# A graph layer and a top-p attention layer on one core: tile ends newest first in the tail, one search cut moved from ACT to DVE, three adjacency loads held back by a memset

## The chip, the cores and the metric

The kernel runs on one core of one Trainium2 chip. The metric is the device time of one execution in microseconds, the median of the runs shown. Engines are named as in the profile: PE (TensorE, with its weight loads PEld), ACT (ScalarE), DVE (VectorE), POOL (GpSimd), SP (SyncE, which here only issues DMAs).

## The reference

Node features `x` are 3327 x 256 in f32, and `adj` is a 3327 x 3327 matrix of zeros and ones with about four ones to a row. Two layers follow each other, each with a layernorm over its sum with its input.

```python
# layer 0: attention over neighbours, then a GRU cell
Wh  = h @ W
e   = leaky_relu(Wh @ a[:F] + (Wh @ a[F:]).T, 0.2)
att = softmax(where(adj > 0, e, NEG_INF), axis=1)
gi, gh = (att @ Wh) @ w_ih.T + b_ih, h @ w_hh.T + b_hh
...                                     # r, z, n of a GRU cell
x = layernorm(x + (1 - z) * n + z * h)

# layer 1: two steps of top-p attention beside a fixed propagation R
R = adj + eye(N); R = R / R.sum(-1, keepdims=True)
Xf = Xa = X = x
for n in range(2):
    A  = top_p_attention(Xa, W1, W2, W3)   # softmax of a 64-wide bilinear form, largest
                                           # entries of a row up to a sum of 0.9, renormalised
    Xf = R @ Xf
    Xa = A @ Xa
    Z  = Z + Xf @ U1[n].T + Xa @ U2[n].T
x = layernorm(X + layernorm(X + Z) * ln_g + ln_b)
```

The second argument `S` of layer 1 is `adj`. So `R @ Xf` is a gather of a few neighbours per row, while the attention is dense: 3327 logits per row, of which the largest up to nine tenths of the row's sum are kept.

## The kernel before, in words

Rows are handled in 26 tiles of 128 (`NT`), the last of 127. `P` is 128, `D` 256.

**Layer 0.** `run` (L1035 on) first projects all tiles (`project`, up to L768): x is loaded and turned, multiplied by W, and the result is stored to DRAM by ACT's queue as `whx`, the table that later gathers read. `ds` (L763) is the last POOL instruction of a tile there. Beside the projection the rows of `adj` are loaded and searched. `load_adj(t, queue)` (L807) brings tile t into one of three arrays `ad[t % 3]` in two transfers, three blocks of 832 columns (1248 KB) and one of 831 (415 KB). `neighbours(t)` (L814) finds the ones with FIND_INDEX8 on DVE (L819); when a tile has been searched, tile t + 3 goes on the list `wanted`. `advance` (L1056) is one phase of the written-out order: it runs some finds, issues one wanted load on SP if the phase is above `NT - EARLY` = 13, opens a tile every sixth phase (`EVERY`) and moves every open tile one step. `tile` (from L840) takes the neighbour lists of a tile, computes where its edges lie (`half` L868, `square` L870, `mid` L875, `edge` L908) and gathers five blocks of 128 rows of `whx` (L613) before attention and GRU.

**Layer 1.** An item is a tile in a step, 52 in all. `product` (L1731) multiplies the masked attention of item i with Xa, seven groups of four 128-wide blocks; behind each group the functions put in a slot (`slot(g, f, ...)`) are issued, which is how logits, exponentials, search and mask of the coming item are woven in. The order on PE, ACT, DVE and in layer 0 on POOL is the order of issue in the program; the remaining instructions are ordered by a scheduler with priorities from the program order.

A row whose list of largest candidates doesn't suffice is "left over": its position, bias and sums are stored (`left_over`, L1531), and three sets of up to 128 such rows, "hard sets" 0, 1 and 2, are worked off at the end. The parts of a hard set k:

- `hard_load` (L1536) loads its rows' numbers and gathers its inputs (L1552).
- `hard_q` (L1558) makes its query on PE and ACT (L1563, L1565) and a first upper threshold `top` (L1571).
- `hard_exp` (L1574) makes its 3327 exponentials.
- `coarse_bound` (L1587) lowers `top` once for each cut factor: four ACT passes over half a row each (L1602), then eight small POOL instructions (L1608 to L1617, the next cut's L1597).
- `bound` (L1621) does the same on DVE: one pass of `kept_sum` (L1341) and three small instructions per cut (L1629, L1632, L1634).
- `hard` (L1638) is the search proper on DVE: one pass (L1644), 20 MAX8 (L1213), a sort, three drops with MATCH_REPLACE8 (L1335), one pass (L1673) and the reciprocal `rA` (L1676). It has eight yields.
- `hard_end` (L1679) is the attention product and the output of the set, mainly PE.
- `hard_store` (L1706) scatters the 128 finished rows to the output (L1708).

The six cut factors are `CUTS` = 1/16, 1/4, 1/2, 0.71, 0.84, 0.92. Sets 1 and 2 use the first three (`COARSE`) coarsely on ACT and the others on DVE; set 0 uses two on ACT and four on DVE.

**The tail.** `ends` (L1744) begins behind the last product. `tile_end(t)` (L1462) turns and multiplies the four propagated inputs of a tile on PE (L1181, L1440), adds x through an identity product (L1492), and hands the PSUM tile to `output_rows` (L1445): a copy to `h` (L1448), two layernorms, each with `moments` on DVE (L1383, L1385) and POOL (L1386, L1387) and three ACT instructions (L1393 to L1395), and two POOL instructions between them (L1453, L1455). The buffers `h`, `x1`, `xb` are twelve slots of 256 columns in the memory of `qT`, no longer needed. `tick()` opens one tile end and moves every open one on by one step, oldest first. `more()` moves the head of `queue` (start or end of a hard set), runs a tick, and gives each coarse bound two steps. The search of the sets is the loop of `ends`: for k = 0, 1, 2 the bounds, then `hard(k)`, with one `more()` at each yield; when all sets are through, `more()` runs until nothing is left.

Of the kernel before, what the change touches and what calls it, by code (L numbers as in the profile page):

```python
# [9 lines left out]
F32 = mybir.dt.float32  # L10
# [6 lines left out]
P = 128  # L17
# [630 lines left out]
class Layer0:  # L648
# [186 lines left out]
    def tile(self, t):  # L835
# [25 lines left out]

        nc.gpsimd.tensor_scalar(info[:r, 0:1], info[:r, 0:1], 1.0, None, ALU.max)
        yield from to(2)
        pst = self.ps.tile([P, 512], F32, tag="sm", name=f"pst{t}")
        nc.tensor.matmul(pst[:, 0:1], sh.lower16, d16, start=True, stop=True)
# [4 lines left out]
        nc.gpsimd.tensor_scalar(square, d1, d1, 0.25, ALU.mult, ALU.mult)  # L870
        nc.gpsimd.tensor_copy(a[:, :MAXDEG], info[:, :MAXDEG])
# [163 lines left out]
    def run(self):  # L1035
# [20 lines left out]
        def advance(finds):  # L1056
            nonlocal phase
            for _ in range(finds):
                find()
            if self.wanted and phase > NT - EARLY:  # L1060
                self.load_adj(self.wanted.pop(0), nc.sync)
            if phase % EVERY == 0 and phase // EVERY < NT:
                tiles.append(self.tile(phase // EVERY))
            for g in list(tiles):
                if next(g, True):
                    tiles.remove(g)
                    self.done += 1
            next(logits, None)
            phase += 1
# [53 lines left out]
class Layer1:  # L1123
# [321 lines left out]
    def output_rows(self, pz, terms, h, r, tag):  # L1445

        nc = self.nc
        nc.scalar.copy(h, pz[:r, :D])  # L1448
        yield
        m = self.moments(h, r, f"a{tag}")  # L1450
        yield
        self.normalized(h, h, m, r, f"a{tag}")
        nc.gpsimd.tensor_tensor(h, h, self.g[:r], ALU.mult)  # L1453
        for term in terms:
            nc.gpsimd.tensor_tensor(h, h, term, ALU.add)  # L1455
        yield
        yield
        m = self.moments(h, r, f"b{tag}")
        yield
        self.normalized(h, h, m, r, f"b{tag}")  # L1460

    def tile_end(self, t):  # L1462
# [3 lines left out]
        a = self.work.tile([P, EB, P], F32, tag="m", name=f"xfs{t}").rearrange("p b c -> p (b c)")  # L1466
        xa2 = self.work.tile([P, D], F32, tag="xf", name=f"xa2_{t}")

        spare = lambda k: sh.qT[:r, k * D : (k + 1) * D]
        h, x1, xb = spare(t % 6), spare(6 + t % 3), spare(9 + t % 3)  # L1470
        move_rows(nc.sync, a[:r, :D], sh.xf_rows[on, :], r)
# [13 lines left out]
        yield  # L1485
        move_rows(nc.sync, xb, sh.xb_rows[on, :], r)
        yield from self.output_rows(pz, [xb], h, r, f"t{t}")
        move_rows(nc.sync, self.out[on, :], h, r)
# [68 lines left out]

    def hard_q(self, k):  # L1558
        nc, v = self.nc, self.items[f"h{k}"]
        xt = self.transposed((v.x[:, 0, :],), P, f"q{v.tag}")  # L1560
        pq = self.psm.tile([P, 512], F32, tag="sm", name=f"pq{v.tag}")
        for c in range(DC):
            nc.tensor.matmul(pq[:, :P], self.sh.wq[:, c, :], xt[:, c, :], start=(c == 0), stop=(c == DC - 1))  # L1563
        v.q = self.work.tile([P, DC, P], F32, tag="xtq", name=f"q{v.tag}")[:, 0, :]
        nc.scalar.copy(v.q, pq[:, :P])  # L1565

        v.p = (*self.more, self.p[0])[k]
# [19 lines left out]
    def coarse_bound(self, k, cuts, junk):  # L1587
# [6 lines left out]
        for f in cuts:  # L1594
# [22 lines left out]
            nc.gpsimd.tensor_tensor(nxt, up, v.top, ALU.mult)  # L1617
            v.top = nxt
            yield

# [123 lines left out]
    def ends(self, bounds):  # L1744


        ends, open_ends, queue = [self.tile_end(t) for t in range(NT)], [], []

        def tick():

            if ends:
                open_ends.append(ends.pop(0))
            for g in list(open_ends):
                if next(g, True):
                    open_ends.remove(g)
# [11 lines left out]
        def start(k):  # L1767
            self.hard_q(k)
            for pair in self.chunks():
# [7 lines left out]

        queue.append(start(2))
        for k in range(HARD):
            if k:  # L1780
# [4 lines left out]
            for _ in self.hard(k):  # L1785
                more()
            queue.append(end(k))
        while queue or open_ends or ends:
            more()
# [3 lines left out]
    def run(self):  # L1793
        nc, sh, total = self.nc, self.sh, STEPS * NT
        self.items = {}
        with self.tc.manual_schedule(
# [14 lines left out]
            for i in range(total):  # L1811
# [169 lines left out]
```

## Time and profile before

| | |
|---|---|
| median of three runs | 1848.85 us (1848.53 to 1852.39) |
| the profiled execution | 1848.5 us; its span 1846.6 us, clock 0.960 |
| busy in the span | PE 1654.3 us (90%), DVE 1314.9 (71%), POOL 1148.5 (62%), ACT 1030.2 (56%) |
| layer 0 | from 0 to about 415 us |
| layer 1, step 0 and step 1 | about 415 to 985 and 985 to 1593 us |
| the tail (`ends` and the stores) | about 1593 to 1846.6 us |

A table of stages gives busy microseconds of each engine in a stretch, with the number of instructions. A line of waits reads: engine, tile and line that waited, what it waited for, microseconds in total, times, longest. A timeline line gives start, duration, engine, line, operation, out <- in, and in brackets the idle time before it and who ended it. Hard sets have an h at the end of their tiles' names, tile ends a t; `at` and `bt` are the first and second layernorm of a tile end; `qT` in the tail is the memory of `h`, `x1` and `xb`.

### The profile page before, as it was taken

The page shows a single profiled execution, that of the slowest core. Times are in us where ns is not written, and L with a number is a line of the kernel's source. Part 1 is how long each engine was busy: PE and PEld are TensorE (multiplying, and loading weights), DVE is VectorE, ACT ScalarE, POOL GpSimd, SP SyncE. Part 2 cuts the span into 40 slices and gives each one's busy share as a digit, 9 for nine tenths or more (in the row PEclk, how much of TensorE's full clock was granted, in tenths as well). Part 3 has the DMA queues.
Part 4 walks back from the last instruction along what each step waited for, and adds up shares of the span by engine and source line. Part 5 has one row for each costly group of instructions (what it writes and reads, how often), then busy time and mean ns, then how long its engine had stood idle before and what let it go on. Part 6 is the DMA issues. An engine that isn't in the chain of part 4 may idle for free. (4 is left out here: it accounts for less than half of the span.)

```text
span 1846.6 us, 27541 instructions
## 1 busy us (share of the span) xinstructions
PE 1654.3 (90%) x8093; PEld 1215.7 (66%) x8093; DVE 1314.9 (71%) x4095; ACT 1030.2 (56%) x2373; POOL 1148.5 (62%) x1908
## 2 busy tenths in 40 slices
PE   6489998969999999999996999999999988679994
PEld 5355555647677777777774777777777656568873
DVE  5788887455555656655546999999999876585872
ACT  3366666646565555555654555555555546677563
POOL 1578777557886666666654556566565572455854
PEclk9799999979999999999998999999999998889997
DMA  9776672222221111111101111111111120122330
GB/s 312 259 251 221 219 218 70 58 63 82 79 58 41 41 41 43 47 47 45 43 26 40 46 50 51 49 55 51 52 49 49 49 63 18 42 76 92 118 98 29
DMA packets 95097, 154.20 MB, mean 84 GB/s; under 512 B 16470, under 2 KB 68173, under 8 KB 94940
## 3 DMA queue, kind: packets, MB, share of 16 engines
q1 hardware_dynamic: 63818, 86.51, 14.4%
q0 software_dynamic: 20384, 53.28, 10.9%
q10 hardware_dynamic: 10738, 12.58, 2.1%
q8 instruction: 66, 1.08, 0.3%
q14 instruction: 91, 0.75, 0.1%
HBM read 124.65 MB, written 27.75 MB: 83 GB/s over the span
## 5 line engine op out<-in xcount | busy, mean ns | idle before, releaser
L1420 PE MATMUL pav<-xa,at 128*128 128x256 f32 (+2 forms) x1352 | 331.8, 390 | 8.8 <-ACT at L1406 8.8
L1406 ACT COPY at<-pt 128x512 f32<-128x512 f32 (+2 forms) x364 | 191.9, 541 | 262.1 <-PE pt L1404 261.4
L1420 PE MATMUL pav<-x,at 128*128 128x256 f32 (+2 forms) x1352 | 325.7, 385 | 7.7 <-ACT at L1406 7.6
L1420 PEld LDWEIGHTS pav<-xa,at 128*128 128x128 f32 (+2 forms) x1352 | 246.5, 192 | 89.8 <-ACT at L1406 43.0
L1420 PEld LDWEIGHTS pav<-x,at 128*128 128x128 f32 (+2 forms) x1352 | 244.4, 190 | 72.5 <-ACT at L1406 28.8
L1200 ACT COPY array<-pl 128x416 f32<-128x416 f32 (+4 forms) x405 | 183.1, 503 | 180.3 <-PE pl L1197 180.2
L1213 DVE MAX8 cand<-array 128x8 f32<-128x167 f32 (+5 forms) x921 | 239.1, 336 | 44.4 <-ACT array L1200 44.4
L613 POOL DMA_INDIRECT g<-xf_rows,edge x130 | 136.4, 1049 | 158.2 <-PE pxf L1366 125.9
L613 POOL DMA_INDIRECT g<-x_rows,edge x130 | 140.4, 1080 | 103.9 <-PE ptq L626 71.0
L1197 PE MATMUL pl<-kT,qT 64*128 64x416 f32 (+4 forms) x810 | 198.0, 560 | 4.5 <-ACT x L1585 2.7
L1305 DVE TENSOR_TENSOR_SCAN before<-e 128x40 f32<-128x40 f32 (+3 forms) x52 | 14.9, 286 | 226.7 <-ACT e L1298 226.7
L1358 POOL TENSOR_SCALAR m<-col,erow 128x128 f32<-128x128 f32 x260 | 162.6, 639 | 14.6 <-PE pxf L1366 8.0
L613 POOL DMA_INDIRECT g<-whx,edge x130 | 141.1, 1085 | 43.9 <-issue 36.1
L1366 PE MATMUL pxf<-g,m 128*128 128x256 f32 (+1 forms) x520 | 133.6, 406 | 15.1 <-POOL m L1358 8.5
L1366 PEld LDWEIGHTS pxf<-g,m 128*128 128x128 f32 (+1 forms) x520 | 98.8, 199 | 69.8 <-issue 41.3
L1231 DVE MAX8 lst<-cand 128x8 f32<-128x160 f32 (+3 forms) x364 | 114.6, 315 | 9.0
L1404 PE MATMUL pt<-ident,array 128*128 128x128 f32 (+1 forms) x676 | 101.1, 276 | 7.1 <-DVE array L1321 7.1
L819 DVE FIND_INDEX8 at<-ones,array 128x8 uint32<-128x840 f32 (+1 forms) x104 | 105.5, 1027 | 0.0
L1404 PE MATMUL pt<-ident,p 128*128 128x128 f32 (+2 forms) x676 | 100.3, 274 | 3.9 <-DVE p L1321 3.9
L1404 PEld LDWEIGHTS pt<-ident,array 128*128 128x128 f32 (+1 forms) x676 | 85.0, 144 | 24.8 <-PE pxf L1366 7.9
L1404 PEld LDWEIGHTS pt<-ident,p 128*128 128x128 f32 (+2 forms) x676 | 84.7, 144 | 21.3 <-PE pxf L1366 7.6
L1321 DVE SCALAR_TENSOR_TENSOR array<-array,t,array 128x3327 f32<-128x3327 f32 x26 | 96.0, 3691 | 0.5
(467 smaller groups left out, 3282.6 us busy)
## 6 DMA issues: line engine op xcount, KB each, us to landing
array<-in_adj_dram SPq DMA_DIRECT2D x23, 1248.0 KB, 6.6
array<-in_adj_dram SPq DMA_DIRECT2D x23, 415.5 KB, 6.7
xf_rows<-xf SPq DMA_DIRECT2D x50, 128.0 KB, 1.7
xa_rows<-xa SPq DMA_DIRECT2D x50, 128.0 KB, 1.7
xfs<-xf_rows SPq DMA_DIRECT2D x50, 128.0 KB, 2.2
whx<-table ACTq DMA_DIRECT2D x25, 129.5 KB, 6.6
x_rows<-x ACTq DMA_DIRECT2D x25, 128.0 KB, 1.7
xb_rows<-xb SPq DMA_DIRECT2D x25, 128.0 KB, 1.7
```

Of the source, the lines that this page charges most:

```text
L613: self.nc.gpsimd.indirect_dma_start(out=dst[:, b, :], out_offset=None, in_=table[:, :], in_offset=bass.IndirectOffsetOnAxis(ap=self.edge[: ...
L819: nc.vector.max_index(at[:r, g, :], self.ones8[:r], ad[:r, g, :])
L1197: nc.tensor.matmul(pl[:r, :w], q[on], self.sh.kT[on, n, s : s + w], start=True, stop=True)
L1200: nc.scalar.copy(l[:r, h * HALF + s : h * HALF + s + w], pl[:r, :w])
L1213: self.nc.vector.max(cand[:r, g * 8 : g * 8 + 8], src[:r, g * group : min(N, (g + 1) * group)])
L1231: nc.vector.max(lst[:r, k : k + 8], cand[:r])
L1321: nc.vector.scalar_tensor_tensor(v.p[:r], v.l[:r, :N], v.t[:r], v.p[:r], ALU.is_ge, ALU.mult, accum_out=sA[:r])
L1358: nc.gpsimd.tensor_scalar(v.m[:, b, :], sh.col1, sh.erow[:, v.at, b : b + 1], None, ALU.is_equal)
L1366: nc.tensor.matmul(acc[:r, :D], v.m[:, b, :r], v.g[:, b, :], start=(b == 0), stop=(b == EB - 1))
L1404: nc.tensor.transpose(pt[: rows(j), j - j0, :r], v.p[:r, cols(j)], self.ident[:r, :r])
L1406: nc.scalar.copy(at[:, :full, :r], pt[:, :full, :r])
L1420: nc.tensor.matmul(v.acc[: v.r, :D], at[:k, j - 4 * g, : v.r], V[:k, j, :], start=(j == 0), stop=(j == NT - 1))
```

## The change

- In `tile` of layer 0, `half` and `square` are issued a step earlier, ahead of the matmul, and the maximum on `info` behind it.
- The loads of `adj` tiles 3, 4 and 5 write an array whose first column POOL has just set to zero by a memset. Only the transfer of three blocks touches that column.
- Set 0 has one coarse cut on ACT and five passes on DVE. Its passes start in slot 0 of the last product, and set 1's first coarse cut in slot 1 rather than 3.
- `hard_q` is issued in three parts, in three slots, or in three ticks for set 2. A coarse cut has two more yields.
- While the sets are searched, tile ends are opened at 0.8 a tick, and open tile ends are moved newest first. `output_rows` has a yield more ahead of each of its moments and one more behind the first.
- `h` has nine slots, `x1` moves to a buffer of its own, and `xb` is loaded two steps later.

```diff
@@ tile, layer 0
-        nc.gpsimd.tensor_scalar(info[:r, 0:1], info[:r, 0:1], 1.0, None, ALU.max)
+        half = ...; square = ...
         yield from to(2)
         pst = self.ps.tile([P, 512], F32, tag="sm", name=f"pst{t}")
         nc.tensor.matmul(pst[:, 0:1], sh.lower16, d16, start=True, stop=True)
-        half = ...; square = ...
+        nc.gpsimd.tensor_scalar(info[:r, 0:1], info[:r, 0:1], 1.0, None, ALU.max)
@@ advance
-            if self.wanted and phase > NT - EARLY:
-                self.load_adj(self.wanted.pop(0), nc.sync)
+            if self.wanted and (self.wanted[0] > 5 or phase > NT - EARLY):
+                t = self.wanted.pop(0)
+                if t <= 5:
+                    nc.gpsimd.memset(self.ad[t % 3][:, 0, 0:1], 0.0)
+                self.load_adj(t, nc.sync)
@@ output_rows
         nc.scalar.copy(h, pz[:r, :D])
         yield
+        yield
         m = self.moments(h, r, f"a{tag}")
         yield
+        yield
         self.normalized(h, h, m, r, f"a{tag}")
...
         m = self.moments(h, r, f"b{tag}")
         yield
+        yield
         self.normalized(h, h, m, r, f"b{tag}")
@@ tile_end
+        x1 = self.work.tile([P, D], F32, tag="xf2", name=f"x1_{t}")[:r]
-        h, x1, xb = spare(t % 6), spare(6 + t % 3), spare(9 + t % 3)
+        h, xb = spare(t % 9), spare(9 + t % 3)
...
-        move_rows(nc.sync, xb, sh.xb_rows[on, :], r)
-        yield from self.output_rows(pz, [xb], h, r, f"t{t}")
+        rest = self.output_rows(pz, [xb], h, r, f"t{t}")
+        for k, _ in enumerate(rest):
+            if k == 2:
+                move_rows(nc.sync, xb, sh.xb_rows[on, :], r)
+            yield
@@ hard_q: a yield behind the transposes, one behind the copy of q
@@ coarse_bound: three yields instead of one behind a cut
@@ ends
+            ticks += 1
-            if ends:
+            if ends and (NT - len(ends) < 0.8 * ticks or not searching):
                 open_ends.append(ends.pop(0))
-            for g in list(open_ends):
+            for g in open_ends[::-1]:
...
         def start(k):
-            self.hard_q(k)
+            yield from self.hard_q(k)
...
+        searching = True      # ahead of the loop over the sets, and False behind it
@@ run
-                if i == total - 4:
-                    slot(6, self.hard_q, 0)
-                if i == total - 2:
-                    slot(3, self.hard_q, 1)
+                for k, at, first in ((0, total - 4, 4), (1, total - 2, 1)):
+                    if i == at:
+                        q = self.hard_q(k)
+                        for g in range(3):
+                            slot(first + g, next, q, None)
...
-                if total - 2 <= i:
-                    coarse = self.coarse_bound(0, CUTS[i - total + 2 :][:1], self.l[0][:, :N])
-                    for g in (0, 1, 2, 3) if i == total - 2 else (0, 0, 1, 1):
+                if i == total - 2:
+                    coarse = self.coarse_bound(0, CUTS[:1], self.l[0][:, :N])
+                    for g in (0, 1, 2, 3):
                         slot(g, next, coarse, None)
...
-                    bound = self.bound(0, CUTS[2:])
+                    bound = self.bound(0, CUTS[1:])
-                    for g in (2, 3, 4, 5, 6):
+                    for g in (0, 1, 2, 3, 4, 5):
                         slot(g, next, bound, None)
-                    for g in (3, 4, 5, 6):
+                    for g in (1, 2, 3, 4):
                         slot(g, next, bounds[0], None)
```

More of the change, by code (lines that the diff above doesn't have):

```diff
@@ L860, in tile @@
         nc.gpsimd.tensor_copy(d16, d1)
-        nc.gpsimd.tensor_scalar(info[:r, 0:1], info[:r, 0:1], 1.0, None, ALU.max)
-        yield from to(2)
-        pst = self.ps.tile([P, 512], F32, tag="sm", name=f"pst{t}")
-        nc.tensor.matmul(pst[:, 0:1], sh.lower16, d16, start=True, stop=True)
         half = self.small("half", f"half{t}")
@@ L870, in tile @@
         nc.gpsimd.tensor_scalar(square, d1, d1, 0.25, ALU.mult, ALU.mult)
+        yield from to(2)
+        pst = self.ps.tile([P, 512], F32, tag="sm", name=f"pst{t}")
+        nc.tensor.matmul(pst[:, 0:1], sh.lower16, d16, start=True, stop=True)
+        nc.gpsimd.tensor_scalar(info[:r, 0:1], info[:r, 0:1], 1.0, None, ALU.max)
         nc.gpsimd.tensor_copy(a[:, :MAXDEG], info[:, :MAXDEG])
@@ L1560, in hard_q @@
         xt = self.transposed((v.x[:, 0, :],), P, f"q{v.tag}")
+        yield
         pq = self.psm.tile([P, 512], F32, tag="sm", name=f"pq{v.tag}")
@@ L1565, in hard_q @@
         nc.scalar.copy(v.q, pq[:, :P])
+        yield
         v.p = (*self.more, self.p[0])[k]
@@ L1618, in coarse_bound @@
             v.top = nxt
+            yield
+            yield
             yield
@@ L1747, in ends @@
         ends, open_ends, queue = [self.tile_end(t) for t in range(NT)], [], []
+        ticks = 0
         def tick():
-            if ends:
+            nonlocal ticks
+            ticks += 1
+            if ends and (NT - len(ends) < 0.8 * ticks or not searching):
                 open_ends.append(ends.pop(0))
-            for g in list(open_ends):
+            for g in open_ends[::-1]:
                 if next(g, True):
@@ L1787, in ends @@
             queue.append(end(k))
+        searching = False
         while queue or open_ends or ends:
```

## The prediction

> **What bounds the kernel now.** I read the slices of the page first: PE is at 9 tenths almost everywhere, so work taken off another engine in the middle buys nothing. It falls to 6 and 7 around 1600 us, and to 4 and 3 in the last two slices; at the start (6 and 4) it waits for loads. The change touches those places alone, so I read the waits of each.
>
> Table by stage, for the tail (columns: span, busy us and instructions of PE, PE loads, DVE, ACT, POOL, then clock, DMA share, GB/s):
>
> ```profile
> 1550.00:1600.00 50.00, 37.86 (x175) 28.00 (x173) 21.24 (x38) 34.49 (x57) 24.17 (x47) 0.90 0.15 33
> 1600.00:1650.00 50.00, 36.14 (x176) 29.05 (x176) 47.38 (x99) 38.92 (x63) 22.20 (x45) 0.89 0.23 71
> 1650.00:1700.00 50.00, 43.99 (x218) 38.02 (x219) 24.60 (x61) 32.81 (x73) 30.23 (x52) 0.90 0.23 72
> 1700.00:1750.00 50.00, 48.22 (x263) 41.66 (x262) 45.12 (x93) 30.48 (x81) 41.08 (x62) 1.00 0.39 114
> 1800.00:1847.00 47.00, 21.50 (x107) 17.94 (x107) 10.92 (x27) 14.90 (x41) 19.35 (x31) 0.78 0.09 28
> ```
>
> No engine is full for 100 us from 1550 on, and DVE alternates between 21 and 47 of 50: a serial search that stops and starts. Waits 1560 to 1610, then 1650 to the end:
>
> ```profile
> DVE cndh L1629 <- POOL toph_0.25_16249 L1617: 19.9, 1, 19.9
> ACT array L1602 <- POOL minush_0.25_16392 L1597: 7.7, 1, 7.7
> PE pqh L1563 <- ACT xtqh L1183: 3.5, 1, 3.5
> ...
> DVE bnat L1383 <- ACT qT L1448: 27.1, 7, 10.0
> DVE bnah L1383 <- ACT xh L1448: 12.3, 2, 7.2
> DVE bnbt L1383 <- POOL qT L1455: 12.2, 5, 8.8
> ```
>
> DVE sits 19.9 us for one number, the second cut that ACT and POOL make for hard set 0. Later it stops at `bn` of tiles whose `h` isn't copied yet, with the search queued behind. DVE timeline, start of set 0's passes, start of its search, last number of set 2's search; then POOL, the third store:
>
> ```profile
> 1590.05 0.15 DVE L1629 TENSOR_SCALAR cndh<-toph_0.25_16249 128x1 f32<-128x1 f32 x1 [19.91 <-POOL toph_0.25_16249 L1617]
> 1607.56 3.68 DVE L1644 SCALAR_TENSOR_TENSOR array<-x,toph 128x3327 f32<-128x3327 f32 x1
> 1806.34 0.16 DVE L1676 RECIPROCAL rAh<-rAh 128x1 f32<-128x1 f32 x1
> 1842.73 0.97 POOL L1708 DMA_INDIRECT out_dram<-xh,idxh  x1 [2.19 <-issue]
> ```
>
> So the tail is a DVE chain: passes 17.5 (to 1607.6), search 0 35.0 (to 1642.5), stage 1 86.5 (to 1729), stage 2 77.3 (to 1806.3). Only then can PE start set 2's end (22.5, to 1828.7), then 7 of row work, then three serial stores (10.4). Beside it PE does 26 tile ends; back to back they start 5.26 us apart (L1440 at 1706.64 and 1711.90), 0.24 of it a wait that other PE work can fill: 5.0 each.
>
> **What the skill says.** The Trainium skill, "SBUF — State Buffer", section "Who interferes with whom": a DVE instruction with two SBUF inputs contends with a GpSimd instruction that reads SBUF, and the second waits for the first's end. The trace agrees: under the pass at 1594.67 a POOL TENSOR_SCALAR (L1614) took 3.56 us, 0.31 elsewhere; under MATCH_REPLACE at 1797.85 POOL stays at 0.19 to 0.73. "DMA: Bandwidth & Descriptors", "Issuing engines are not separate DMA queues": transfers of all issuers share the same 16 DMA engines. The trace agrees: DMA share 0.95 and 308 GB/s in the first 50 us, with ACT's stores stuck behind adj. The same page's anatomy gives a transfer some 2.0 us of fixed cost; the output stores here wait 2.25 and 2.19.
>
> **The change, part by part.**
>
> *adj tiles 3 to 5.* The 3-row-block part (1248 KB each) now waits for a POOL memset in phases 14 to 16; the 415 KB part still goes early. Waits of 0 to 70 us:
>
> ```profile
> DVE at L819 <- DMA array<-in_adj_dram: 12.3, 3, 6.7
> ACT mid L875 <- DMA array<-in_adj_dram: 3.9, 1, 3.9
> ACT xT L754 <- DMA array<-in_adj_dram: 2.2, 1, 2.2
> ```
>
> ACT's 2.2 and 3.9 are its own store issues behind adj transfers; they go, so the projection (last L763 at 62.9) ends some 6 us sooner. Against it: the memset of tile 3 stands on POOL about 1.2 us after the last L763, its load takes 6.6 (page part 6), so it lands about 8 us after that point, where before FIND_INDEX8 of tile 3 ran 4.3 after. DVE waits some 4 us, and it is only 1.2 us ahead of POOL's next edge; a whole tile on POOL is 9.9 to 11.3 us (five gathers), the bound of layer 0 from 68 us on. Tiles 4 and 5 follow a gather apart and cost at most 1. SP: the loads waiting for POOL have only later loads behind them. Sum 6 − 4 = 2 sooner, between 2 slower and 4 faster.
>
> *half and square ahead, max behind.* Same count, three POOL ops of about 0.2 moved before the next edge and gathers. Once (7.2 us longest of "ACT mid <- POOL half") ACT waits less; but POOL's dense gathers bound this stage: 0, at most 0.6 late per tile if `edge` slips, hidden by 0.3 to 0.5 gaps.
>
> *Second cut of set 0.* Gone: four ACT passes of 1.69+0.19 = 7.5 us and eight POOL ops. Added: a fifth DVE pass, 4.36 us (1590.05 to 1594.48). The first cut's number is ready on POOL at 1567.6 and DVE is free at 1570.1, so passes run 1570.2 + 5 × 4.36 = 1592 rather than 1607.5: **15.5 sooner**, of which I keep 14.5, since POOL ops under the passes stretch. Those ops are the index of set 2 (four), xf's sum, set 1's eight of cut 1: about three fit between two passes. Set 2's gathers (1580 to 1588) may slip by 6, needed only tens of us later.
>
> *hard_q in three slots, start(2) two ticks later.* PE's in-line 4.3 and 3.5 at 1554 and 1590 go: up to 7.8 on PE; in the first case DVE's mask sets the pace, so I count them in PE's balance only.
>
> *Set 1's cut earlier, two yields more per cut.* The 7.66 of ACT at 1595 to 1602 (POOL locked twice by passes) and PE's 8.5 behind it go, as set 0's search (MAX8, one input) doesn't lock. Six nexts per cut and two per tick: three ticks per cut; cuts 2 and 3 need six of the search's eight ticks. Just fits.
>
> *Tile ends.* Newest first, 0.8 a tick, moments two ticks after the copy instead of one. Each of the search's 30 ticks (8+3+8+3+8) opens 0.8, so 24 are open by the end, two are left. Stage 1: passes 3 × 4.4 = 13.2, search 34, 18 moments × 0.62 = 11: 58 of DVE work, where before took 86.5 with 25.6 of listed waits. I leave 9: 67. Stage 2: 59 and 6: 65 (77.3 with 16). Then search 0 from 1593, 36 → 1629, → 1696 → **1761** against 1806.3: 45 sooner. Does PE follow? From 1590 to 1761 it has two set ends of 20, logits, and some 22 tile ends × 5.0 = 110: about 158, plus 10 idle until the first `h`: yes, with nothing to spare.
>
> *After the search.* PE has set 2's end (20) and about four tile ends (20): 40 instead of 22.5. The last tile's row work is 13 instead of 7, being up to 12 ticks of one chain on ACT, DVE and POOL; stores 11 with the landing. 1761 + 40 + 13 + 11 = 1825.
>
> *Slots of h, x1 in its own buffers, xb later.* Nine against six slots: an `h` lives 12 ticks × 0.8 = 9.6 openings, so a slot is just free or a copy waits for a store. xb and x1 are 128 KB loads (2 us), at 0.39 DMA share: 0; at worst the copy waits a tick, 4 us once.
>
> **Sum**, against the profiled execution (1848.5; span 1846.6 and 1.9 around it; median of runs 1848.85): 1825 − 2 + 1.9 = 1825, on the median's footing 1825.5; I say 1826. A floor: PE's remaining work from 1590 is 60 + 130 + 8 = 198 with no idle → 1788 + 11 + 11 = 1810 with the end.
>
> **Rivals.**
>
> 1. *The end grows more than the search shrinks (slower).* After search 2, PE 40 for 22.5 and row work 13 for 7: +24. If DVE's waits (25.6 and 16) stay, because PE at 5.0 per tile and not the order makes `h` late, only the 14.5 of the start remains: 1806.3 − 14.5 + 64 = 1856, and the same with layer 0's −2 and the 1.9. It decides when search 2 ends later than about 1785 (1785 + 64 = 1849). For it: PE is at 48 of 50 in 1700 to 1750 already. Against: newest first puts a wait on a tile just copied nowhere; moments come two ticks later.
>
> 2. *ACT and POOL replace the wait.* Set 1's cuts (8 × 1.88 = 15), set 2's exp (4.4) and copies give ACT 37 to 45 us in search 0's 35, with POOL behind locks before it: search 1 starts 8 to 14 late. 1838. For: ACT at 38.9 of 50 already.
>
> 3. *The held load is late for layer 0:* POOL shifts by 4 to 8, the tail as forecast: 1832.
>
> 4. *The change doesn't do what it says:* the 20 us go, but half of the later waits stay, search 2 ends near 1784, and the end takes it all back: 1848.
>
> **Numbers.** Forecast 0.60 (1811 to 1835), rival 2 0.17, 3 0.05, 4 0.07, 1 0.11. A measurement can tell about 0.2%, 3.7 us. Faster: 0.60 + 0.05 + 0.15 = 0.80; slower 0.12 with a part of 4; same 0.08. Range 1809 to 1849: out are rival 1, the top of 4 and 0.05 below.
>
> **What would show it.** DVE at L1629 near 1570 with no 19.9 wait, L1644 first at about 1592; five passes. `bnat <- qT` from 27 to under 10; the last L1676 at about 1760 (over 1784: rival 1). Then PE busy 40 us, L1708 from about 1814. The last gather of layer 0 (L613 `g<-whx`, 350.5 us now) some 2 earlier; `L819 <- DMA` not over 12.3. Wrong if DVE waits for `toph_0.5` of set 1 over 8 us (rival 2), or if a POOL gather waits for an edge near 70 us (rival 3).

## The result and the profile after

The changed kernel takes 1846.8 us (median of 12 runs, 1843.9 to 1850.4) beside 1848.5 us for the kernel before (12 runs, 1843.5 to 1852.4). The ratio is 0.9994 with a 95% interval of 0.9982 to 1.0007: no change that can be told. The forecast was 1826, 1809 to 1849. The time lies inside that range, but it didn't fall as forecast.

The profiled execution of the changed kernel took 1845.05 us, its span 1843.2 us. Inside, the tail has changed a great deal. The DVE timeline, at the first pass of set 0, the first instruction of its search and the last number of set 2's search; then PE's last product of a tile end:

```profile
1564.00 0.16 DVE L1646 TENSOR_SCALAR cndh<-toph_0.0625_16118 128x1 f32<-128x1 f32 x1 [0.57 <-POOL toph_0.0625_16118 L1631]
1586.55 3.68 DVE L1661 SCALAR_TENSOR_TENSOR array<-x,toph 128x3327 f32<-128x3327 f32 x1
1769.99 0.16 DVE L1693 RECIPROCAL rAh<-rAh 128x1 f32<-128x1 f32 x1
...
1809.45 0.60 PE L1503 MATMUL pzt<-x,ident 127*127 127x256 f32 x2
```

The wait of 19.9 us is 0.57, search 0 starts 21 us sooner, search 2 ends 36 us sooner, and PE has its last product 18.6 us sooner (1810.1 against 1828.7). The span ends only 3.4 us sooner. POOL's timeline says where the rest is. These are the first and the last of the three scatter stores:

```profile
1832.47 1.14 POOL L1725 DMA_INDIRECT out_dram<-xh,idxh  x1 [4.28 <-DMA out_dram<-qT]
...
1839.28 0.97 POOL L1725 DMA_INDIRECT out_dram<-xh,idxh  x1 [2.20 <-issue]
```

From PE's last product to the first store it is 22.4 us; before it was 7.5. The last 3.3 of the 22.4 are the last tile's own store: its second layernorm ends at 1829.15, and the scatter waits until that store has landed. The stages of 50 us (columns as before):

```profile
1550.00:1600.00 50.00, 38.45 (x185) 29.78 (x183) 44.46 (x83) 27.84 (x49) 34.20 (x38) 0.91 0.21 54
1600.00:1650.00 50.00, 42.52 (x211) 34.96 (x212) 37.57 (x61) 35.58 (x62) 25.15 (x42) 0.92 0.19 59
1650.00:1700.00 50.00, 43.55 (x219) 37.10 (x218) 35.37 (x97) 38.50 (x85) 30.84 (x74) 0.97 0.31 94
1700.00:1750.00 50.00, 47.02 (x256) 41.03 (x255) 38.24 (x100) 25.87 (x69) 33.78 (x43) 1.00 0.32 97
1800.00:1847.00 47.00, 9.14 (x44) 7.23 (x42) 6.27 (x24) 18.06 (x54) 20.99 (x38) 0.65 0.13 43
```

DVE's busy time moved from later windows into the first (21.2 to 44.5). In the last window PE does 9 us instead of 21.5, while ACT and POOL do more than before (18.1 and 21.0 against 14.9 and 19.4). The kernel now ends on row work with PE idle. The waits, 1650 to the end:

```profile
DVE bnbt L1387 <- POOL qT L1461: 26.9, 12, 3.6
...
DVE bnat L1387 <- ACT qT L1452: 14.8, 4, 7.8
DVE bnah L1387 <- ACT xh L1452: 11.2, 3, 5.2
```

The wait for the copy of `h` fell from 27.1 to 14.8. A rise of 14.7 in `bnbt` stands beside it; 18.5 of its 26.9 us lie behind the search, where DVE has nothing else to do.

### The profile page after: what moved, and what is told of

It reads as the page before. It is cut to its first block, busy times and chain, and to the rows that moved or that the text cites. A ratio compares the mean times of both kernels' runs of the same rounds, so it can differ in the third digit from the quotient of the medians.

```text
span 1843.2 us, 27552 instructions
## 1 busy us (share of the span) xinstructions
PE 1642.9 (89%) x8093; PEld 1210.1 (66%) x8093; DVE 1317.1 (71%) x4100; ACT 1022.7 (55%) x2365; POOL 1157.2 (63%) x1902
## 3 DMA queue, kind: packets, MB, share of 16 engines
q1 hardware_dynamic: 63818, 86.51, 14.4%
## 5 line engine op out<-in xcount | busy, mean ns | idle before, releaser
L613 POOL DMA_INDIRECT g<-xf_rows,edge x130 | 136.5, 1050 | 156.4 <-PE pxf L1370 124.1
L613 POOL DMA_INDIRECT g<-x_rows,edge x130 | 139.9, 1076 | 104.0 <-PE ptq L626 71.2
L1309 DVE TENSOR_TENSOR_SCAN before<-e 128x40 f32<-128x40 f32 (+3 forms) x52 | 14.4, 276 | 224.2 <-ACT e L1302 224.2
L1362 POOL TENSOR_SCALAR m<-col,erow 128x128 f32<-128x128 f32 x260 | 162.8, 640 | 14.5 <-PE pxf L1370 8.0
L613 POOL DMA_INDIRECT g<-whx,edge x130 | 141.3, 1087 | 46.3 <-issue 36.1
L1370 PE MATMUL pxf<-g,m 128*128 128x256 f32 (+1 forms) x520 | 133.0, 404 | 14.7 <-POOL m L1362 8.0
```

Of the source, the lines that this page charges most:

```text
L613: self.nc.gpsimd.indirect_dma_start(out=dst[:, b, :], out_offset=None, in_=table[:, :], in_offset=bass.IndirectOffsetOnAxis(ap=self.edge[: ...
L1362: nc.gpsimd.tensor_scalar(v.m[:, b, :], sh.col1, sh.erow[:, v.at, b : b + 1], None, ALU.is_equal)
L1370: nc.tensor.matmul(acc[:r, :D], v.m[:, b, :r], v.g[:, b, :], start=(b == 0), stop=(b == EB - 1))
```

## The experiments

Chips and executions differ ahead of the tail: in the traces the last gather of step 1 starts between 1514.0 and 1530.1. So besides the ratio to the kernel before, which ran on the same chip, I give the **tail**: in the profiled execution, from the start of the last gather of step 1 (L613 `g<-xf_rows`) to the end of the span. It is 327.3 us before (1846.6 − 1519.3) and 325.2 after (1843.2 − 1518.0). "End of search 2", "PE's end" and "stores" are counted from that gather too: 287.0, 309.4 and the first store at 316.9 before; 252.0, 292.1 and 314.5 after. Two runs that leave the tail as it is (e5, e6) have tails of 325.3 and 325.0.

One difference between executions lies inside this count. In the profiled executions of f1, h1 and h2 the stretch from that gather to the last product, which no edit touches, was some 3.1 us longer than in the changed kernel (f5: 1.7), at a lower granted clock. Here are the changed kernel and f1, with the same 285 products:

```profile
1518.00:1580.00 62.00, 57.56 (x285) 43.31 (x284) 50.29 (x118) 43.04 (x77) 29.38 (x46) 1.00 0.13 31
1521.60:1586.70 65.10, 60.75 (x285) 45.15 (x284) 50.33 (x118) 43.02 (x77) 29.32 (x46) 0.95 0.13 29
```

So for these runs take 3.1 (f5: 1.7) off "end of search 2", "PE's end" and "tail" in the table when comparing with the changed kernel; the text below says where it matters. In e1 and f4 some output rows are wrong (see there), and their times are only a guide.

| kernel | ratio (95% interval) | end of search 2 | PE's end | PE's end to first store | tail |
|---|---|---|---|---|---|
| before | 1 | 287.0 | 309.4 | 7.5 | 327.3 |
| after | 0.9994 (0.9982 to 1.0007) | 252.0 | 292.1 | 22.4 | 325.2 |
| cut alone (e4) | 0.9991 (0.9981 to 1.0002) | 287.1 | 309.6 | 7.5 | 327.6 |
| after without the cut (e7) | 1.0033 (1.0017 to 1.0049) | 258.6 | 298.8 | 23.0 | 332.2 |
| oldest first (e3) | 1.0016 (1.0008 to 1.0024) | 258.5 | 295.9 | 24.4 | 330.8 |
| nine ticks (h1) | 1.0008 (0.9997 to 1.0019) | 266.4 | 303.1 | 18.0 | 331.6 |
| 1.0 a tick (e2) | 1.0033 (1.0021 to 1.0046) | 281.4 | 308.8 | 9.5 | 328.9 |
| 0.6 a tick (h2) | 1.0032 (1.0022 to 1.0042) | 236.5 | 301.4 | 22.4 | 333.8 |
| short rows (e1) | 0.9966 (0.9952 to 0.9980) | 251.9 | 291.8 | 19.4 | 321.7 |
| two steps a tick (f2) | 0.9965 (0.9948 to 0.9982) | 252.0 | 292.3 | 17.3 | 320.2 |
| finer set ends (f1) | 0.9932 (0.9918 to 0.9945) | 251.6 | 291.8 | 12.7 | 315.3 |
| before, finer set ends (b1) | 0.9968 (0.9957 to 0.9979) | 282.3 | 308.2 | two stores ahead | 321.6 |
| f4: finer, short, layer 0 | 0.9915 (0.9890 to 0.9941) | 250.1 | 293.0 | 9.3 | 313.4 |
| f5: finer, two steps, layer 0 | 0.9887 (0.9861 to 0.9914) | 251.4 | 295.0 | one store ahead | 308.4 |

### The cut, with and without the new tile ends

**e4_cut_only.** The kernel before with set 0's cut moved and nothing else:

```diff
-                if total - 2 <= i:
-                    coarse = self.coarse_bound(0, CUTS[i - total + 2 :][:1], ...)
-                    for g in (0, 1, 2, 3) if i == total - 2 else (0, 0, 1, 1):
+                if i == total - 2:
+                    coarse = self.coarse_bound(0, CUTS[:1], ...)
+                    for g in (0, 1, 2, 3):
...
-                    bound = self.bound(0, CUTS[2:])          # slots 2 to 6; set 1's cut 3 to 6
+                    bound = self.bound(0, CUTS[1:])          # slots 0 to 5; set 1's cut 1 to 4
```

> The kernel before with only the cut of set 0 moved: one coarse cut on ACT, five passes on DVE in slots 0 to 5, set 1's first coarse cut in slots 1 to 4. Search 0 starts 17 to 20 us sooner than 1607.5. If the DVE chain bounds the tail of the kernel before, the time falls by most of that, to 1830 to 1836. If PE bounds it (its end can fall only by its idle time), search 2 ends 8 to 12 sooner and the time is 1838 to 1844. If the waits for h take the place of the wait removed, 1846 to 1849.

Search 0 starts 14.9 us sooner against the gather (73.4 against 88.3) and nothing arrives: 0.9991, the tail 327.6. The waits of DVE inside search 0 (1598 to 1644):

```profile
DVE bnat L1383 <- ACT qT L1448: 9.8, 3, 7.5
```

Search 0 takes 45.4 us instead of 34.9, stage 1 takes 90.8 instead of 86.4, and search 2 ends where it did. The wait for a cut has become a wait for `h`, the third of the cases on record.

**e7_no_cut.** The changed kernel with that edit undone.

> The changed kernel with set 0's second coarse cut back on ACT and its passes and set 1's cut in their old slots; the new tile ends stay. Alone on the old tile ends the new cut moved nothing (0.9991). If the cut counts only together with the new tile ends, because these take DVE's waits out of the search, search 2 ends 15 to 20 us later than in the changed kernel against the end of step 1, PE's end moves by 5 to 12 and the time is 6 to 12 us over the changed kernel. If PE's fixed work bounds the tail whatever the search does, PE's end moves by under 3 and the time is that of the changed kernel.

The ratio goes to 1.0033, 0.4% over the changed kernel's; search 2 ends 6.6 us later and PE 6.7 later, and the tail is 7.0 longer. I had expected 15 to 20 us later for the search, and 5 to 12 for PE. So the cut counts only with the new tile ends, and then 7 us of the 16.5 by which it starts search 0 sooner. Stage 1 gives back the other 9.6: it takes 71.7 us here and 81.3 in the changed kernel. DVE comes earlier to tile ends that aren't ready.

### Who makes the search wait

**h2_pace_06.** `0.8 * ticks` becomes `0.6 * ticks`: fewer tile ends run beside the search, ACT's coarse passes stay.

> The changed kernel with 0.6 instead of 0.8 tile ends opened per tick. If PE's work per tick is what DVE waits for in stage 1, the waits fall from 24 to 10 to 14 and search 2 ends 15 to 20 us sooner (1750 to 1755), while about 9 tile ends instead of 4 are left behind it: PE ends where it did within 5, the row work behind it stays at 15 to 25 us, and the time is the changed kernel's within 6. If DVE's waits come from ACT's coarse passes instead, they stay at 20 or more, search 2 gains under 6, and the time rises by 5 to 15.

DVE's waits of stage 1 (first the changed kernel, 1620 to 1703, then this one, 1620 to 1712):

```profile
DVE bnat L1387 <- ACT qT L1452: 8.6, 2, 7.3
DVE bnbt L1387 <- POOL qT L1461: 7.2, 4, 3.5
DVE bnah L1387 <- ACT xh L1452: 5.2, 1, 5.2
```

```profile
DVE bnah L1387 <- ACT xh L1452: 5.4, 1, 5.4
DVE bnat L1387 <- ACT qT L1452: 5.3, 2, 4.6
DVE bnbt L1387 <- POOL qT L1461: 4.4, 4, 2.1
```

All of DVE's waits in stage 1 fall from 24.1 to 16.6, less far than the 10 to 14 expected, and four norms fewer stand in its queue (14 instead of 18, 2 us). Stage 1 falls from 81.3 to 71.1, stage 2 from 67.8 to 59.3, and search 2 ends 15.5 us sooner, 18.7 with the 3.1 of the clock taken off. So it is the work of the tile ends that DVE waits for, not ACT's coarse passes. The run takes PE's, ACT's and POOL's share of that work away together. That PE's share is the one that counts is likely but not shown: 14.2 of the changed kernel's 24.1 us of waits end between 1644 and 1658, and PE is busy for 25.0 of the 25.6 us from 1639.4 to 1665. The time rises all the same: behind search 2 PE has 64.9 us left instead of 40.1 and ends 9.3 later (6.1 without the clock), further than I had expected, and the 22.4 us of row work come on top.

**e2_pace_one.** `1.0 * ticks`, the old pace.

> The changed kernel with 1.0 instead of 0.8 tile ends opened per tick of the search. Theory A: all 26 are open before search 2 ends, PE has only the set's end left there (20 to 25 us instead of 40), the search itself ends 5 to 15 us later since its ticks carry more PE work; the last tile's norms are done under set 2's end, so the store starts 8 us behind PE's end: 1832 to 1840. Theory B: PE's end stays at 1808 to 1812 and the time at 1843 to 1848.

A miss: 1.0033. The row work behind PE does shrink to 9.5 us, as I had said, but search 2 ends 29 us later (stages of 90.0 and 88.5), and PE's end, not the row work, is late by 17. The tile ends are used up before the search is: in the 17 us ahead of search 2's end PE is busy for 6.8. A pace of 0.8 lies between the two losses.

**e3_oldest_first.** `for g in list(open_ends)` again.

> The changed kernel with open tile ends moved oldest first again. If newest first is what keeps DVE's waits for h small in the search, search 2 ends 5 to 15 us later than 1770 and the time is 1846 to 1855. If newest first is what delays the last norms (ACT works on the newest tile and the older ones' second norms queue behind), the store starts 5 or more us sooner: 1838 to 1842. Theory B: no change, 1846.

Search 2 ends 6.5 us later, all of it through stage 1 (86.6) and stage 2 (69.0). Newest first is worth that much of the search, and 0.2% of the time. Behind PE's end it is 24.4 instead of 22.4: the order isn't what makes the row work long.

**h1_nine_ticks.** The three extra yields in `output_rows` are gone, and xb is loaded at the copy (`k == 0`).

> The changed kernel without the three extra yields in output_rows at any time: nine ticks of row work per tile as before the change, newest first and 0.8 a tick kept, xb loaded at the copy of h. Theory A2 (what is left of the last tiles' steps when PE ends sets the time): the work behind PE's end falls from 22.4 to 14 to 18 us. If the extra yields are also what keeps DVE's waits for h down, stage 1's waits rise from 24 to over 30 and search 2 ends 5 to 12 later, and the two cancel: within 3 us of the changed kernel. If they don't matter for the waits, 5 to 8 us below it.

Both halves hold. Row work behind PE's end falls to 18.0, the upper end of what I expected; DVE's waits in stage 1 rise to 29.2, just under the 30 expected, and the stage to 87.1. Search 2 ends 14.4 later than in the changed kernel, 11.3 with the clock taken off, and the ratio is 1.0008, on the "cancel" side. The longer row work does serve the search; the trouble is what it leaves behind it.

### What stands behind PE's end

ACT behind PE's last product in the changed kernel, from its timeline, the copy of the last tile's `h` and what follows on ACT:

```profile
1810.08 0.37 ACT L1452 COPY qT<-pzt 127x256 f32<-127x256 f32 x1 [1.01 <-PE pzt L1503]
1810.35 0.21 ACT L1397 ACTIVATE shiftat<-mvat 128x1 f32<-128x1 f32 x1
1810.65 0.29 ACT L1398 ACTIVATE shiftat<-shiftat,mvat 128x1 f32<-128x1 f32 x1
1810.98 0.60 ACT L1399 ACTIVATE qT<-qT,shiftat,mvat 128x256 f32<-128x256 f32 x1
...
1818.16 0.19 ACT L1397 ACTIVATE shiftat<-mvat 127x1 f32<-127x1 f32 x1
...
1828.55 0.60 ACT L1399 ACTIVATE qT<-qT,shiftbt,mvbt 127x256 f32<-127x256 f32 x1
```

The last tile's `h` is copied at 1810; its first layernorm begins on ACT at 1818 and its second ends at 1829. Each norm costs ACT 1.1 us, and those of the other open tiles and of set 2 stand between, in order. Yet ACT had time: in steps of 20 us (columns as in the stages above),

```profile
1770.00:1790.00 20.00, 19.76 (x110) 17.37 (x109) 4.20 (x15) 9.18 (x23) 9.85 (x21) 1.00 0.25 73
1790.00:1810.00 20.00, 18.98 (x100) 16.09 (x99) 2.67 (x11) 9.80 (x27) 4.53 (x10) 1.00 0.06 20
1810.00:1830.00 20.00, 0.16 (x3) 0.06 (x2) 4.21 (x15) 13.43 (x40) 14.12 (x28) 0.57 0.19 61
```

it is half idle while PE is full, and POOL at least half. Row work goes one step per tick, and a tick of a set's end is some 10 us of PE. Counted from the yields, PE's 40 us behind the search are four ticks, and the last tile's last step is in the thirteenth: nine ticks of row work, of several tiles at once, are left when PE ends.

**f1_fine_ends.** The changed kernel, one edit in `hard_end`:

```diff
-            if g % 2:
-                yield
+            yield
```

> The changed kernel, but hard_end yields behind each of its seven groups instead of every second, so a set's end takes eight ticks of about 2.5 to 5 us of PE instead of four of 10. Theory A2 (row work is counted in ticks, the ticks of a set's end are 10 us of PE each, so only four of the last tiles' twelve steps are done when PE ends and eight are left): behind PE's last work 10 to 14 us instead of 22.4, and fewer waits of the search for h in stage 1 (24 to about 15): 1830 to 1838. Theory B (PE's idle of 25 us behind 1590 is all that counts, and it isn't moved): the time stays within 3 us of the changed kernel.

It gives 0.9932, the tail 315.3, 9.9 us less (13 with the clock taken off). 9.7 us of it are behind PE's end, 12.7 instead of 22.4. Search 2 and PE end where they did in the table (within 0.4 us); with the clock taken off, both end some 3.5 us sooner; the search's part comes from stage 1, which takes 76.7 instead of 81.3. PE's work behind the search now fills eight ticks, and the last tile's products stand among the set's groups, 11.2 us ahead of PE's end, where in the changed kernel they come last. PE's timeline, the last product of the last tile and of set 2:

```profile
1801.59 0.60 PE L1503 MATMUL pzt<-x,ident 127*127 127x256 f32 x2
...
1812.34 1.06 PE L1503 MATMUL pzh<-xh,ident 128*128 128x256 f32 x2
```

So the edit shortens the ticks and, by that, brings the last tile forward; no run separates the two. In POOL's timeline the first store now follows set 2's own row work, no longer a tile's store:

```profile
1825.03 0.55 POOL L1391 TENSOR_TENSOR mvbh<-mvbh,power 128x1 f32<-128x1 f32 x1
1826.10 1.14 POOL L1724 DMA_INDIRECT out_dram<-xh,idxh  x1 [0.52 <-issue]
```

Stage 1's waits fell only from 24.1 to 20.4, less than I had expected.

**f2_double_steps.** Behind the search, `for _ in range(1 if searching else 2)` around the loop over the open tile ends.

> The changed kernel, but once the search is over each open tile end moves two steps per tick. Theory A2: eight of the last tiles' steps fit under set 2's end, 22.4 us behind PE's end become 10 to 14, if PE doesn't stall in order for ACT: time 8 to 12 us below the changed kernel. If the in-order ACT queue (copies of set 2's end behind norms that wait for DVE and POOL) holds PE, PE ends 5 to 10 us later and the gain is 0 to 4. The search ends where it does in the changed kernel (1770).

The other way to get more row steps under PE's work: 17.3 us behind PE's end instead of 22.4, PE's end unmoved (0.2), 0.9965. The time gains some 5 us, where I expected 8 to 12. I take it, without a run for it, that the second step of a tick waits for the first in the in-order queues.

**e1_short_rows.** The extra yields only while the search runs (`if self.searching: yield`). The edit leaves out one thing: with fewer yields, xb is loaded at the wrong place in the order. Tiles 21 to 25 here, and tiles 19 and 20 in f4, add the xb of another tile, so these rows are wrong. The instructions are as many and as long, but these additions don't wait for their own load.

> The changed kernel, but the three extra yields in output_rows are taken only while the sets are searched. Theory A (the search ends 36 us sooner, and the gain is spent behind PE's last work, because a tile's row work takes twelve ticks and its norms pile up on ACT and POOL): PE ends near 1810 as in the changed kernel, the first set's store starts 8 to 13 us later instead of 22.4, time 1833 to 1839. Theory B (PE's fixed work in the tail sets the end and row work only fills in): 1846 as before. Theory C (the ticks behind the search are too few in any case; twelve or nine doesn't matter, what counts is that the last tiles open late): 1842 to 1845.

19.4 us behind PE's end: 3 us, not the 9 to 14 of theory A. Its gain of 0.28%, some 5 us, is what theory C had at most. Taking steps away from twelve helps less than making the ticks short, which is the difference between theory A here and the one of f1.

**b1_before_fine.** The same edit of `hard_end` on the kernel before.

> The kernel before with the one edit of hard_end, a yield behind each group. Behind its search only set 2's end is left and 7.5 us of row work, so nothing is to be had there. If long ticks of PE also make the search wait for h (25.6 us in stage 1, 16.6 in stage 2), search 2 ends 5 to 10 us sooner and the time falls by as much: 0.994 to 0.998. If the search waits for PE's sum of work, not for its grain, no change: 0.999 to 1.001.

0.9968. Search 2 ends 4.7 us sooner, just under the range I had given. The rest I hadn't seen: the stores. POOL's timeline has two of them before set 2's row work is done:

```profile
1831.64 1.14 POOL L1707 DMA_INDIRECT out_dram<-xh,idxh  x1 [6.28 <-DMA out_dram<-qT]
1835.06 0.98 POOL L1707 DMA_INDIRECT out_dram<-xh,idxh  x1 [2.27 <-ACT xtwh L1183]
1844.78 1.07 POOL L1707 DMA_INDIRECT out_dram<-xh,idxh  x1 [1.25 <-ACT xh L1395]
```

PE's end to the end of the span is 13.4 us instead of 17.9. So an edit worth 0.3% was to be had before the change, through the waits and the stores; behind the change it is worth 0.6%, through the row work.

### Layer 0

**e6_no_hold.** The changed kernel without the memset that holds back tiles 3 to 5.

> The changed kernel without the memset that holds back adj tiles 3 to 5. If the held loads gave the 8.4 us sooner start of the gathers (62.1 minus the 3.1 wait, against 68.1), the first edge goes back from 58.6 to about 67, the second edge comes at 77 to 78 instead of 74.8, and the last gather at 353 to 354, so 3 us slower in all. If the hold only moved the wait (POOL's gather behind the load, DVE behind tile 3), the last gather stays at 351 and the time is the same.

The first edge (L908) comes at 69.2 instead of 58.6, the second at 80.2 instead of 74.8, the last at 348.1 instead of 343.5: 4.6 us in this pair of traces. The other traces say how far that holds. The projection's last L763 is at 54.5 to 56.9 in the twelve with the hold and at 62.3 to 64.7 in the four without, so the projection does end sooner with it. Of that, some 2.5 us are left in the mean at edge 5, counted from 0 (118.0 against 120.5, but only 0.4 on the chip of e1 to e4). The ratio is 1.0009 (1.0000 to 1.0019) beside 0.9994 (0.9982 to 1.0007): the two intervals overlap. In the changed kernel the waits of 0 to 70 us are

```profile
DVE at L819 <- DMA array<-in_adj_dram: 15.0, 4, 7.3
...
POOL g L613 <- DMA array<-in_adj_dram: 3.1, 1, 3.1
```

so the first edge, 8.4 us sooner than in the kernel before (58.55 against 66.95), loses 5.5 again by the second: DVE waits 3.3 and 3.1 us for held tiles, and POOL's first gather stands 3.1 us, which the profile puts down to an adj load.

**e5_half_back.** The changed kernel with `half`, `square` and the maximum in their old order.

> The changed kernel with half, square and the maximum of layer 0's tile back in their old order. In the traces the gap between two tiles' edges is 0.12 us longer in the changed kernel from tile 5 on. If the order of the three POOL instructions is what costs that, the last whx gather comes 2 to 3 us sooner (348 to 349, against 350.9) and the time falls by as much, if the tail carries it. If the 0.12 has another cause (where the first gather stands against the others), the last gather stays at 350 to 351.

The last whx gather comes at 348.3 instead of 350.9 and the ratio is 0.9975 (0.9966 to 0.9983), 0.19% under the changed kernel's, whose interval just overlaps. The tail doesn't differ (325.3). The traces are clearer: from edge 5 to edge 25 it is 226.0 to 227.2 us in all ten with the new order and 223.8 to 224.7 in all six with the old one. The same tile in POOL's timeline, before the change and after it, between the first gather and the next norm:

```profile
143.12 0.21 POOL L868 TENSOR_SCALAR half<-d 128x1 f32<-128x1 f32 x1
143.29 0.31 POOL L870 TENSOR_SCALAR square<-d 128x1 f32<-128x1 f32 x1
143.50 0.23 POOL L871 CAST tell<-info 128x16 bf16<-128x16 f32 x1
143.81 0.23 POOL L872 TENSOR_TENSOR tell<-info,tell 128x16 bf16<-128x16 f32 x1
144.02 0.19 POOL L996 TENSOR_SCALAR mv<-mv 128x1 f32<-128x1 f32 x1
```

```profile
141.26 0.26 POOL L870 TENSOR_SCALAR info<-info 128x1 f32<-128x1 f32 x1
141.59 0.20 POOL L871 CAST tell<-info 128x16 bf16<-128x16 f32 x1
141.87 0.22 POOL L872 TENSOR_TENSOR tell<-info,tell 128x16 bf16<-128x16 f32 x1
142.06 0.19 POOL L996 TENSOR_SCALAR mv<-mv 128x1 f32<-128x1 f32 x1
```

Two instructions moved out of this stretch and one in, and it is only 0.10 shorter (0.90 to 0.80), while the stretch ahead of the edge grew by 0.22: the maximum is now followed at once by a cast that reads its result, and starts 0.33 apart from it, where `half` and `square`, which don't read each other, started 0.17 apart. That is the 0.12 us per tile, and over 20 tiles (edge 5 to edge 25: 226.7 against 224.2 in e5) 2.5 us. That the order costs this is shown; that reading the neighbour's result is the reason is only read from these lines.

### Both kinds together

**f4_fine_short_half** and **f5_fine_double_half.** The finer set ends and layer 0's old order, with e1's short rows (xb loaded sooner) or with f2's two steps.

> The changed kernel with three edits together: a yield behind each group of hard_end, the extra yields of output_rows only while the sets are searched (xb then loaded a step earlier), and layer 0's three POOL instructions in their old order. If the gains add (about 9 from the first against the changed kernel, 2.6 from the last, 2 to 5 from the second), 1830 to 1834 on a chip where the kernel before takes 1850, ratio 0.989 to 0.992; row work behind PE's end 8 to 11 us. If the first edit has already taken what the second could give, 0.9915 to 0.993 and 12 us.

> The changed kernel with a yield behind each group of hard_end, two steps per tick for the open tile ends once the search is over, and layer 0's old order. If row steps under set 2's end are what is short, 8 to 10 us behind PE's end and a ratio of 0.988 to 0.991. If two steps a tick make ACT's copies for set 2's end wait behind norms, PE ends 3 to 8 later and the ratio is 0.991 to 0.994.

f4 gives 0.9915, f5 0.9887 (0.9861 to 0.9914): 1831.8 us median where the kernel before takes 1854.0. f5 is the fastest of these versions and beats both kernels. Its PE ends 2.9 us later than the changed kernel's (1.2 with the clock taken off). It waits for ACT to scale set 2's product, which stands behind the tiles' norms in ACT's queue,

```profile
PE ptxwh L1185 <- ACT xa_h L1435: 5.5, 1, 5.5
```

but all tiles are stored before set 2 is done. The first of the three stores leaves at 1813.7, ahead of PE's end at 1815.3, and PE's end to the end of the span is 13.4 us against 33.1 in the changed kernel.

No run takes back by itself `hard_q` in three parts, the two more yields of a coarse cut, or the new buffers of `h`, `x1` and `xb`.

## Why the prediction was wrong

The forecast's sum put the span's end at 1823; it was 1843.2. Two terms of the sum failed: the waits left in the search's stages (17 us, of which an earlier start and search 0 gave back 6) and the row work behind PE (9 us).

- **Start of search 0: right, and more, with one step wrong.** Forecast 14.5 kept of 15.5; it starts 21.0 sooner, of which 1.3 lie ahead of the tail. e7 puts the edit itself at 16.5. (The passes' 4.36 us is right for the second to fourth; the first, whose ends the working quotes, is 4.43.) But the working had set 2's gathers slip by 6 us and "needed only tens of us later". They took 3.9 to 4.3 us each under the passes instead of 1.00, nine more in all, and PE asked for the first at once; set 1's cut stands behind them on POOL, so ACT's wait at that place is 7.8 as before (7.7), and did not go as forecast. POOL's timeline, the first three and the fourth of these gathers, and PE's and ACT's waits of 1550 to 1610:

```profile
1578.42 4.33 POOL L1563 DMA_INDIRECT xh<-xa_rows,idxh  x1 [0.16 <-POOL thrh L1643]
1583.05 3.89 POOL L1563 DMA_INDIRECT xh<-x_rows,idxh  x1 [0.30 <-issue]
1587.25 3.86 POOL L1563 DMA_INDIRECT xh<-xf_rows,idxh  x1 [0.30 <-issue]
1591.41 1.00 POOL L1563 DMA_INDIRECT xh<-xf_rows,idxh  x1 [0.30 <-issue]
```

```profile
ACT array L1616 <- POOL minush_0.25_16425 L1611: 7.8, 1, 7.8
...
PE ptxut L1185 <- ACT xtut L1187: 6.0, 1, 6.0
...
PE ptxqh L1185 <- DMA xh<-xa_rows,idxh: 5.2, 1, 5.2
```

  These 11 us of PE waiting may be part of why stage 1 finds PE no earlier. The kernel without the cut (e7) has some 8 of its own at that place, so most of them are not what the cut adds.
- **Stages 1 and 2: the first step that failed.** Forecast 67 and 65, measured 81.3 and 67.8. I left 9 us of waits in stage 1; there were 24, hardly fewer than before. The working asked whether PE follows and answered "with nothing to spare" for the sum of both stages. It should have asked it for stage 1 alone. In e7 the search starts 16.5 us later and stage 1 takes 9.6 less; in h2 fewer tile ends shorten it by 10.2. So DVE, started earlier, meets tile ends that aren't earlier. Search 2 ended at 1770, not 1759 (the forecast with its layer 0 gain): 11 us.
- **PE behind the search: right.** Forecast 40, measured 40.1.
- **Row work behind PE: the second step that failed.** Forecast 13 for "up to 12 ticks of one chain", measured 22.4. I priced one tile's chain. ACT's and POOL's queues held the norms of the other open tiles as well, as rows advance once a tick and the ticks of a set's end are long, and the last 3.3 us, until the tile's own store has landed, weren't in my sum. f1 shows it by making the ticks shorter: 9.7 of these us vanish.
- **Layer 0: one step of two failed.** The hold I put at 6 − 4 = 2 sooner; the traces have some 2.5 in the mean, 4.6 in the pair of e6. The reordering I priced at nothing, "same count"; e5 has 2.5 slower. With the tail's start within 1.3 us of before, the two leave nothing.
- **The rivals.** Rival 1 had the right mechanism, an end that grows by more than the search shrinks, and its size (+24) was too small: the end grew by 32.9 us, from 40.3 to 73.2 behind search 2. But I let it decide only if search 2 ended later than 1785. It ended at 1770 and the growth ate it still. Rival 4's time, 1848, was nearly the result, for the wrong reason: search 2 wasn't near 1784. Rival 2 is not seen: DVE waits 1.0 us for `toph_0.5` of set 1. Rival 3 is not seen: layer 0 isn't later than before, and e6 without the hold isn't sooner.

The floor that I set, 1810 with no idle of PE, was a floor for one row behind PE: it priced at 11 us what took 22 in the changed kernel.

## What to carry to other kernels

When a schedule advances background work one step per tick, count the ticks: how many fit under the long engine's work where the background work must drain, and what all open chains together still have to do behind it. The latency of one chain is not the price. Take a wait away only after asking what the engine meets next when it comes earlier; e4's 15 us vanished in the next two waits. An instruction moved among others of its engine isn't free because the count is the same: the order alone cost 2.5 us here.

## What the runs showed of the hardware that I had not expected

- An indirect gather on POOL took 3.9 to 4.3 us under DVE's passes over two 3327-wide operands and 1.00 beside them; each of the three ended 0.9 to 1.0 us after the end of the pass that it met. The prediction had this for POOL's arithmetic alone. The Trainium skill, "SBUF — State Buffer", "Who interferes with whom", has the contention for a GpSimd instruction that reads SBUF, but infers that the building of a DMA's descriptors isn't held up by an instruction that takes only the shared read side. These gathers were held up, whichever part of them it was, and here the measurement decides.
- Of two small POOL instructions in a row in layer 0's tile, a pair whose second reads the first's result starts 0.27 to 0.33 us apart (maximum and cast 0.33, square's neighbours cast and subtraction 0.31), several pairs without that 0.14 to 0.21. One pair doesn't fit: the edge starts 0.34 behind square and doesn't read it. This is read from the traces of these pairs; no run measured it by itself. The order alone was worth 0.12 us per tile.
- Holding loads back made the kernel's start faster: with three loads of 1248 KB held until the projection was over, its `whx` stores took 3.9 us from issue to landing in the median (6.6 before, 5.0 in e6), and it ended at 54.5 to 56.9 us instead of 62.3 to 64.7.
- The three scatter stores of the last sets take 10.4 to 10.8 us in a row up to the end of the span (before, after, f1; 2.2 to 2.5 us between two), and 4.5 to 5.1 from the last one's issue to the end when the first two, or one of them, went out sooner (b1, f5).
